# First layers of two pairs of edge blocks in one turn, and another head and end, in a graph network layer on one core

## The chip, the cores and the metric

One core of a Trainium2 chip. PE multiplies matrices into PSUM, DVE (vector) and ACT (scalar) work on tiles in SBUF and PSUM, POOL (GpSimd) here mostly issues gathers from DRAM, SP issues plain DMAs. The metric is the time of one execution on the device in microseconds; lower is better. Before the change it is 2216.37 us, the median of three runs (2215.54 to 2216.93).

## The reference

6250 nodes with 256 features, 206,250 directed edges sorted by target node, an average of 33 per node. Each edge has 64 raw features and one "polarity".

```python
h = relu(layernorm(x))
polarity = clip(edge_attr[:, 0:1], 0, 1)
e = relu(raw @ W_e1.T + b_e1) @ W_e2.T + b_e2            # raw: 64 features
edge_emb = (e * (polarity + 0.01)) @ W_le.T + b_le
msg = relu(h[src] + edge_emb)
aggr = segment_sum(msg, dst)                             # 6250 rows
g = (h + aggr) @ W_g1.T + b_g1
out = x + relu(layernorm(g) * ln_g + ln_b) @ W_g2.T + b_g2
```

All of it is float32. The kernel multiplies W_e2 and W_le into one matrix first (`wc_s`, with `bc_s` for the bias), so each edge passes through a first layer of 64 x 256 and a second of 256 x 256.

## The kernel before

**Tiles.** Edges are laid out in 67 groups of 3072 (6 blocks of 512) and one last group of a single block, 403 blocks in all. Two blocks are a *pair* (202 pairs): their raw features fill 128 partitions, the even block the upper 64 rows, the odd block the lower 64. Half a block, 256 edges, is a *unit* u; there are 806.

**What is done for a pair, and where.**
- `load_pair(q)` (L217): 256 KB of raw features by SP.
- `first_layer(q)` (L222): four matmuls with 64 rows (two blocks, two halves of the 256 features), the two blocks side by side in the upper and lower rows of the array; each result is a PSUM buffer of 128 x 512. It is evacuated with bias and relu by ACT (L241); for the first blocks only (L237), the last of the four goes to DVE (L238). Each matmul in float32 is two instructions on PE, so a first layer is 8 of them.
- `edge_part(u)` (L248): the second layer, four matmuls of 128 x 128 by 128 x 256 (8 instructions); DVE adds `bc_s` into `msg` (L261); a few early units (`plain`) are copied by ACT.
- `gathers` (L495): for each unit two indirect DMAs on POOL fetch the rows of `hb_d` (relu of the normalized x, plus b_le) into `hg`, one of 16 buffers. The first of each batch waits for the second layer's last matmul (`last_z`).
- `whole(u)` (L520): two multiply-adds on DVE (message times polarity plus gathered row, L526), a relu on ACT (L528), in place in `hg`.
- `add_up(b)` (L530): sums over edges with the same target, as matmuls with 0/1 matrices `sel` that have 32 columns; four of them lie side by side in the columns of the array (L536). They gather in `pd`; at the end of a group ACT copies them to `ms` (L542).
- `node_work(w)` (L569) for each of 49 windows of 128 nodes, in steps some units apart: `spread` loads, `ready` (L593) makes the normalized rows, `rows_of` (L599) takes the sums from the groups that touch the window (L607), `one`, `two`, `three` call `first`, `second`, `third` (L158 to L188) of `finish_nodes`.

**Order.** The order is written out by hand (`manual_schedule`): each engine runs its instructions as the program lists them. `forward(u)` (L275) emits the second layer of a unit; in one unit of four (u % 4 == TURN, that is 1) it also calls `turn_of(q)` (L268): the first layer of pair q + 2, then the sums that are due (`add_pairs`), then the load of pair q + 4. So PE goes through second layer (32 instructions), first layer (8), sums (16), and again. `whole` follows the second layer at a distance of 22 units that shrinks by one in every 36 units; `add_pairs` takes pairs whose units are all `whole`.

**PSUM.** Seven buffers `pz` of one bank each rotate among first layer, second layer and node work; `pd` is the eighth.

**Head.** The weights' product, the normalization of all x (in 13 parts: statistics on DVE, scaling on ACT, an add on POOL, stores to `hb_d` by SP) and the first 22 units of both layers run together; then the gathers start. In `todo`, keyed by unit, stand small early jobs: target rows, selection matrices, node weights, and a check of the edges' order whose verdict would send the kernel into a slow general version (`any_order`), which does not run here.

**End.** The last sums, `ms`, then the node work of the last two windows, as one chain.

Of the kernel before, what the change touches and what calls it, by code (L numbers as in the profile page):

```python
# [17 lines left out]
P = 128  # L18
# [23 lines left out]
SHRINK = 36  # L42
HG = 16
TURN = 1
CH = 4
# [46 lines left out]
def gnn_kernel(ctx: ExitStack, tc: tile.TileContext, x, src_c, dst_c, dst_r, pol_c, raw_t, w_e1t, w_e2,  # L92
# [49 lines left out]
    def finish_nodes(nd, ps, w, n):  # L142

        r = w * P

        def turn(a):
            pt = ps()
            for c in range(2):
                nc.tensor.transpose(pt[:, 0, c * P:c * P + n], a[:n, c * P:(c + 1) * P], ident[:n, :n])
            aT = nd.tile([P, 2, P], F32, name="aT")  # L150
            if n == P:
                nc.scalar.activation(aT, pt[:, 0, :].rearrange("p (c n) -> p c n", c=2), AF.Copy)
            else:
                for c in range(2):
                    nc.scalar.activation(aT[:, c, :n], pt[:, 0, c * P:c * P + n], AF.Copy)
            return aT

        def first(aT):  # L158
            ph = ps()
            for c in range(2):  # L160
                nc.tensor.matmul(ph[:n, 0, :], aT[:, c, :n], wg1_s[:, c, :], start=c == 0, stop=c == 1)  # L161
            hs = nd.tile([P, D], F32, name="hs")
            nc.vector.tensor_add(hs[:n], ph[:n, 0, :], bg1_b[:n])
            mv = row_stats(nd, n, 1, lambda i: hs[:n])
            rs = nd.tile([P, 1], F32, name="rs1")
            one_over_std(rs[:n], mv, n)
            nc.vector.tensor_scalar(hs[:n], hs[:n], mv[:n, 0, 0:1], rs[:n], op0=ALU.subtract, op1=ALU.mult)
            return hs

        def second(hs):  # L170
            pt = ps()
            for c in range(2):
                nc.tensor.transpose(pt[:, 0, c * P:c * P + n], hs[:n, c * P:(c + 1) * P], ident[:n, :n])  # L173
            nT = nd.tile([P, 2, P], F32, name="nT")
            for c in range(2):
                nc.scalar.activation(nT[:, c, :n], pt[:, 0, c * P:c * P + n], AF.Relu, bias=lnb_s[:, c:c + 1],  # L176
                                     scale=lng_s[:, c:c + 1])
            return nT

        def third(nT, xt):  # L180
            po = ps()
            for c in range(2):
                nc.tensor.matmul(po[:n, 0, :], nT[:, c, :n], wg2_s[:, c, :], start=c == 0, stop=c == 1)  # L183
            ot = nd.tile([P, D], F32, name="ot")
            nc.vector.tensor_add(ot[:n], po[:n, 0, :], bg2_b[:n])
            nc.vector.tensor_add(ot[:n], ot[:n], xt[:n])
            for a, b in spread_out(n):
                nc.sync.dma_start(out=out[bass.ds(r + a, b - a), :], in_=ot[a:b])  # L188

        def load_x():  # L190
            xt = nd.tile([P, D], F32, name="xt3")
            for a, b in spread_out(n):
                nc.sync.dma_start(out=xt[a:b], in_=x[bass.ds(r + a, b - a), :])
            return xt

        return turn, first, second, third, load_x

# [3 lines left out]
    with fast:  # L201
# [3 lines left out]
        sel_p = big.enter_context(tc.tile_pool(name="sel", bufs=3))  # L205
        e1_p = big.enter_context(tc.tile_pool(name="e1", bufs=6))
        msg_p = big.enter_context(tc.tile_pool(name="msg", bufs=LEAD + 2))
# [14 lines left out]
        def first_layer(q):  # L222
# [12 lines left out]
            for c in range(2):  # L235
                for s, b in enumerate(bs):
                    if b < 2 * LEAD // 4 + 4 and s == c == 1:  # L237
                        nc.vector.tensor_scalar(e1[b][:, c, :], pe[s, c], be1_s[:, c:c + 1], 0.0, op0=ALU.add,  # L238
# [9 lines left out]
        def edge_part(u):  # L248
# [4 lines left out]
            for i in range(2):  # L253
                k = (2 * v + i) * P
                for c in range(2):
                    last_z = nc.tensor.matmul(pz[:, i, :], e1[b][:, c, k:k + P], wc_s[:, c, :], start=c == 0, stop=c == 1)  # L256
            msg[u] = msg_p.tile([P, 2, D], F32, name="msg")
            if plain(u):
# [6 lines left out]
        last_z = None  # L265
        sums = lambda: None

        def turn_of(q):  # L268

            if q + 2 < NP:  # L270
                first_layer(q + 2)
            sums()
            load_pair(q + 4)

        def forward(u):  # L275

            edge_part(u)
            if u % 4 == TURN:
                turn_of(u // 4)

        nc.vector.memset(eps_t, EPS)
        nc.vector.memset(ones, 1.0)
        nc.vector.memset(rs_s, 0.0)
        nc.vector.memset(nm_s, 0.0)
        make_identity(nc, ident)
        warm = const.tile([P, 1], F32, name="warm")
        nc.scalar.activation(warm, eps_t, AF.Sqrt, bias=eps_t)
        vecs = load("vecs", [P, 8], vec_c, nc.scalar)
        be1_s, be2_s, lng_s, lnb_s = (vecs[:, 2 * i:2 * i + 2] for i in range(4))
        load_pair(0)  # L290
        nc.scalar.dma_start(out=we1_s, in_=w_e1t)
        early = ExitStack()
# [17 lines left out]
        with tc.tile_pool(name="p1", bufs=4) as p1, tc.tile_pool(name="p1x", bufs=11) as p1x:  # L310
# [52 lines left out]
            def offset():  # L363
# [5 lines left out]
                nc.scalar.activation(bc_s, pw, AF.Copy)  # L369

            load_rows(0, 2)
            rows_b = const.tile([P, 3, D], F32, name="rows_b")
            nc.scalar.dma_start(out=rows_b, in_=row_v.rearrange("(o r) d -> o r d", o=1).to_broadcast([P, 3, D]))
            ble_b, bg1_b, bg2_b = (rows_b[:, i, :] for i in range(3))
            load_rows(1)
            load_pair(1)
            load_rows(2)
# [9 lines left out]
            for k in range(len(parts) + 1):  # L387
# [19 lines left out]
                if k in lists:  # L407
                    t, src = lists[k]
                    nc.scalar.dma_start(out=t, in_=src[:, :NT])
            for u in units:  # L410
                forward(u)
# [77 lines left out]
        with tc.tile_pool(name="hg", bufs=HG) as hg_p, tc.tile_pool(name="ms", bufs=5) as ms_p, \  # L489
# [30 lines left out]
            def whole(u):  # L520

                m = msg.pop(u)
                if plain(u):
# [6 lines left out]
            def add_up(b):  # L530

                g = group_of(b)
                k = b - g * L
                for j in range(S):
                    m = hg[2 * b + j // 2]
                    nc.tensor.matmul(pd[j * W:(j + 1) * W, g % 2, :], sel[g][:, k * S + j, :], m[:, j % 2, :],  # L536
                                     start=k == 0, stop=b == blocks_of(g)[-1])
                hg.pop(2 * b)
                hg.pop(2 * b + 1)
                if b == blocks_of(g)[-1]:  # L540
                    ms[g] = ms_p.tile([P, D], F32, name="ms")
                    nc.scalar.activation(ms[g], pd[:, g % 2, :], AF.Copy)  # L542
                    sel.pop(g)
# [25 lines left out]
            def node_work(w, spread_now=False):  # L569
# [3 lines left out]

                far_apart = (3, 5, 4) if gs[-1] < NG - 3 else (2, 3, 2)
                turn, first, second, third, load_x = finish_nodes(nd, ps, w, n)

                def spread():
# [7 lines left out]
                    for g in gs:  # L585
# [3 lines left out]
                        box["sel2"].append(s2)  # L589
                    if not spread_now:  # L590
                        at(now + 3, ready)

                def ready():  # L593

                    hT, st = box["hT"], box["st"]
                    for i, op in enumerate((ALU.mult, ALU.add)):
                        nc.vector.tensor_tensor(hT[:, :, :n], hT[:, :, :n], st[:, i:i + 1, :n].to_broadcast([P, 2, n]), op)  # L597

                def rows_of():  # L599

                    if spread_now:
                        ready()
                    hT = box["hT"]
                    pa = ps()
                    for c in range(2):
                        for i, g in enumerate(gs):
                            nc.tensor.matmul(pa[:, c, :n], ms[g][:, c * P:(c + 1) * P], box["sel2"][i][:, :n],  # L607
                                             start=i == 0, stop=i == len(gs) - 1)
                    nc.vector.scalar_tensor_tensor(hT[:, :, :n], hT[:, :, :n], 0.0, pa[:, :, :n], op0=ALU.max, op1=ALU.add)
                    at(now + far_apart[0], one)  # L610

                def one():
                    box["hs"] = first(box["hT"])
                    at(now + far_apart[1], two)
# [21 lines left out]

            gathers(HG)
            nc.vector.tensor_copy(dst_f, dst_f.bitcast(I32))
            sums = add_pairs
            for i, fn in enumerate((first_rows, rows_of_edges, lambda: select(0), lambda: select(1), row_numbers,  # L640
                                    node_weights, stats_out)):
                at(LEAD + i, fn)
            for i, fn in enumerate((by_group(0, ALU.max), by_group(1, ALU.min), by_row(0, ALU.max), by_row(1, ALU.min),
                                    verdict, count, total)):
                at(LEAD + 22 + 2 * i, fn)
            flag = None
            for u in range(LEAD, NU):
                now = u
                forward(u)

                gathers(4 * summed + HG - 4 + (u - TURN) % 4 + 1, last_z)
                while made < u + 1 - max(LEAST, LEAD - u // SHRINK):
                    whole(made)
                    made += 1
                due()
                if u == NU - 10:
                    for w in range(NW):
# [20 lines left out]
def any_order(tc, dram, v):  # L678
# [7 lines left out]
    with tc.tile_pool(name="sc", bufs=1) as sc, tc.tile_pool(name="sk", bufs=2) as sk, \  # L686
# [78 lines left out]
        def nodes(w, n):  # L765
            ac = sk.tile([P, D], F32, name="ac_a")
            nc.sync.dma_start(out=ac[:n], in_=acc_d[bass.ds(w * P, n), :])
            turn, one, two, three, load_x = v["finish_nodes"](sk, lambda: sp1.tile([P, 1, D], F32, name="ps_a"), w, n)
            three(two(one(turn(ac))), load_x())

# [66 lines left out]
```

## Time and profile before

The profiled execution took 2216.74 us, 0.4 above the median; its span, from first to last instruction, is 2214.7 us.

| engine, line | what | times | busy us | mean ns |
|---|---|---|---|---|
| PE L256 | second layer | 6448 | 1477.7 | 382 |
| PE L233 | first layer | 1612 | 403.6 | 617 |
| PE L536 | sums | 3224 | 215.0 | 385 |
| PE L607 | sums to windows | 560 | 70.8 | 275 |
| DVE L526 | message times polarity plus row | 1612 | 703.5 | 477 |
| DVE L261 | bias of the second layer | 799 | 549.6 | 688 |
| ACT L528 | relu of the message | 806 | 511.2 | 634 |
| ACT L241 | evacuation of the first layer | 799 | 483.2 | 686 |
| whole span | | | 2214.7 | |

"Busy" is the time in which at least one instruction of the group was under way, so overlapping matmuls count once while their mean is that of one. The means of PE's rows cannot be multiplied by their number: matmuls in different rows or columns of the array run together, and those that follow each other overlap. What a stretch of PE costs is read from start to start in the timeline. The DMA engines are busy 44% in most of the span, at some 140 GB/s; only in the first fortieth are they full (95%, 307 GB/s). PE's granted clock is 0.998 of full speed over the span.

The page names what ended each idle time; for POOL, whose gathers are each followed by 0.30 us without any instruction, "issue" or whatever engine last signalled is named even when nothing was waited for.

### The profile page before, as it was taken

What the parts mean: (1) busy time and instruction counts of PE and PEld (TensorE: products, weight loads), DVE (VectorE), ACT (ScalarE), POOL (GpSimd) and SP (SyncE); (2) the same over time, 40 slices, a digit from 0 to 9 for tenths busy, and PEclk for the clock granted to TensorE, in tenths of its full rate; (3) what the DMA queues carried; (4) which work ended last, traced back from release to release, by engine and by line L of the source; (5) the groups of instructions that cost most, each with busy time, mean ns of one, the idle gap of its engine ahead of it and who ended that gap; (6) DMA issues with size and microseconds to landing.
All of it is one profiled execution on the core that took longest, in us unless ns stands there. A gap on an engine that the chain in (4) does not pass through costs nothing.

```text
span 2214.7 us, 33981 instructions
## 1 busy us (share of the span) xinstructions
PE 2189.4 (99%) x12360; PEld 1581.9 (71%) x12360; DVE 1477.9 (67%) x3277; ACT 1064.6 (48%) x1895; POOL 1639.9 (74%) x1674
## 2 busy tenths in 40 slices
PE   8999999999999999999999999999999999999998
PEld 6767777777777777777777776777777777777775
DVE  7786666666666666666667666666666666666665
ACT  7444454444444444444444444444444444454443
POOL 5777777777777777777777777777777777777773
PEclk9999999999999999999999999999999999999999
DMA  9544444444544444444444444444344444444442
GB/s 307 159 129 121 151 146 130 139 128 142 149 143 125 131 146 134 151 132 136 141 142 130 150 124 146 131 148 134 115 146 145 119 130 146 140 141 130 139 132 59
DMA packets 156070, 309.13 MB, mean 140 GB/s; under 512 B 33183, under 2 KB 77944, under 8 KB 155896
## 3 DMA queue, kind: packets, MB, share of 16 engines
q0 software_dynamic: 77376, 211.39, 32.5%
q1 hardware_dynamic: 77384, 92.24, 13.2%
q10 hardware_dynamic: 1136, 3.27, 0.5%
q8 instruction: 98, 1.61, 0.3%
q14 instruction: 76, 0.62, 0.1%
HBM read 293.92 MB, written 12.85 MB: 139 GB/s over the span
## 4 chain that ended last, share of the span: by engine, by line
PE 95%; DMA 1%; POOL 1%; DVE 1%; issue 1%; ACT 1%; SPq 0%; ACTq 0%; DVEq 0%
PE pz L256 62%; PE pz L233 17%; PE pd L536 9%; PE pz L607 3%; PE pz L183 2%; PE pz L161 2%; POOL hg L503 1%; DMA hg<-hb_d,src_s 1%; DVE hg L526 1%; PE pz L173 0%; ACT e L241 0%; DMA raw<-in_raw_t_dram 0%; DVE msg L261 0%; DMA wle_s<-in_w_let_dram 0%; ACT hg L528 0%
## 5 line engine op out<-in xcount | busy, mean ns | idle before, releaser
L503 POOL DMA_INDIRECT hg<-hb_d,src_s x1612 | 1604.1, 995 | 516.7 <-issue 350.2
L256 PE MATMUL pz<-wc_s,e 128*128 128x256 f32 x6448 | 1477.7, 382 | 3.4 <-DVE msg L261 1.7
L256 PEld LDWEIGHTS pz<-wc_s,e 128*128 128x128 f32 x6448 | 1200.8, 190 | 240.1 <-issue 49.4
L528 ACT ACTIVATE hg<-hg 128x512 f32<-128x512 f32 x806 | 511.2, 634 | 997.6 <-DVE hg L526 994.4
L261 DVE TENSOR_TENSOR msg<-pz,bc_s 128x512 f32<-128x512 f32 x799 | 549.6, 688 | 655.6 <-PE pz L256 655.3
L526 DVE SCALAR_TENSOR_TENSOR hg<-msg,pol_s,hg 128x256 f32<-128x256 f32 x1612 | 703.5, 477 | 22.5 <-DMA hg<-hb_d,src_s 21.9
L241 ACT ACTIVATE e<-pz,vecs 128x512 f32<-128x512 f32 x799 | 483.2, 686 | 108.0 <-PE pz L233 107.3
L233 PE MATMUL pz<-raw,we_s 64*128 64x512 f32 x1612 | 403.6, 617 | 6.4 <-DMA we_s<-in_w_e1t_dram 4.9
L233 PEld LDWEIGHTS pz<-raw,we_s 64*128 64x128 f32 x1612 | 139.9, 186 | 169.1 <-issue 137.0
L536 PE MATMUL pd<-hg,sel 128*32 128x256 f32 x3224 | 215.0, 385 | 3.9 <-ACT ms L542 3.9
L536 PEld LDWEIGHTS pd<-hg,sel 128*32 128x32 f32 x3224 | 84.5, 109 | 187.6 <-issue 134.8
L607 PEld LDWEIGHTS pz<-s,ms 128*128 128x128 f32 x560 | 70.1, 192 | 3.9 <-ACT ms L542 0.9
L607 PE MATMUL pz<-s,ms 128*128 128x128 f32 (+1 forms) x560 | 70.8, 275 | 0.7 <-ACT ms L542 0.7
L516 DVE TENSOR_TENSOR sel<-iota_w,rel 128x768 f32<-128x768 f32 x68 | 63.8, 938 | 0.0
L347 POOL TENSOR_TENSOR hb<-xt,rows_b 128x256 f32<-128x256 f32 (+1 forms) x49 | 34.2, 732 | 25.4 <-ACT xt L343 17.2
L183 PE MATMUL pz<-wg_s,nT 128*128 128x256 f32 (+1 forms) x196 | 51.4, 386 | 0.0
L161 PE MATMUL pz<-wg_s,hT 128*128 128x256 f32 (+1 forms) x196 | 50.1, 379 | 0.0
L597 DVE TENSOR_TENSOR hT<-hT,stb 128x256 f32<-128x256 f32 (+1 forms) x98 | 41.2, 421 | 1.7
L183 PEld LDWEIGHTS pz<-wg_s,nT 128*128 128x128 f32 (+1 forms) x196 | 37.5, 192 | 6.0 <-PE pd L536 0.4
L161 PEld LDWEIGHTS pz<-wg_s,hT 128*128 128x128 f32 (+1 forms) x196 | 37.1, 190 | 5.1
L176 ACT ACTIVATE nT<-pz,vecs 128x128 f32<-128x128 f32 (+1 forms) x98 | 38.8, 446 | 0.6 <-PE pz L173 0.6
L587 DVE TENSOR_SCALAR s<-iota_p,rowid 128x128 f32<-128x128 f32 x140 | 31.8, 291 | 0.0
(76 smaller groups left out, 326.3 us busy)
## 6 DMA issues: line engine op xcount, KB each, us to landing
raw<-in_raw_t_dram SPq DMA_DIRECT2D x202, 256.0 KB, 3.0
hg<-hb_d,src_s POOLq DMA_INDIRECT x1612
stb<-st_d SPq DMA_DIRECT2D x49, 128.0 KB, 5.6
hb_d<-hb SPq DMA_DIRECT2D x12, 512.0 KB, 5.1
xt<-in_x_dram SPq DMA_DIRECT2D x48, 128.0 KB
hT<-in_x_t_dram SPq DMA_DIRECT2D x48, 128.0 KB
out_dram<-ot SPq DMA_DIRECT2D x48, 128.0 KB, 2.6
xt<-in_x_dram SPq DMA_DIRECT2D x11, 512.0 KB, 9.3
```

Of the source, the lines that this page charges most:

```text
L161: nc.tensor.matmul(ph[:n, 0, :], aT[:, c, :n], wg1_s[:, c, :], start=c == 0, stop=c == 1)
L183: nc.tensor.matmul(po[:n, 0, :], nT[:, c, :n], wg2_s[:, c, :], start=c == 0, stop=c == 1)
L233: nc.tensor.matmul(pe[s, c], we1_s[s * F:(s + 1) * F, c * P:(c + 1) * P], raw[q][s * F:(s + 1) * F, :], start=True, stop=True)
L241: nc.scalar.activation(e1[b][:, c, :], pe[s, c], AF.Relu, bias=be1_s[:, c:c + 1])
L256: last_z = nc.tensor.matmul(pz[:, i, :], e1[b][:, c, k:k + P], wc_s[:, c, :], start=c == 0, stop=c == 1)
L261: nc.vector.tensor_add(msg[u], pz, bc_s)
L503: g = nc.gpsimd.indirect_dma_start(out=hg[u][:, i, :], out_offset=None, in_=hb_d, in_offset=bass.IndirectOffsetOnAxis(ap=src_s[:, 2 * u + ...
L516: nc.vector.tensor_tensor(sel[g][:, :n, :], iota_w.rearrange("p (o w) -> p o w", o=1).to_broadcast([P, n, W]), rel[:, t:t + n].rearrange(" ...
L526: nc.vector.scalar_tensor_tensor(hg[u][:, i, :], m[:, i, :], pol_s[:, 2 * u + i:2 * u + i + 1], hg[u][:, i, :], op0=ALU.mult, op1=ALU.add)
L528: nc.scalar.activation(hg[u], hg[u], AF.Relu)
L536: nc.tensor.matmul(pd[j * W:(j + 1) * W, g % 2, :], sel[g][:, k * S + j, :], m[:, j % 2, :], start=k == 0, stop=b == blocks_of(g)[-1])
L607: nc.tensor.matmul(pa[:, c, :n], ms[g][:, c * P:(c + 1) * P], box["sel2"][i][:, :n], start=i == 0, stop=i == len(gs) - 1)
```

## The change

- **Turns.** For pairs 6 to 195 (`by_two`, `FEW = 6`), a turn with even q does the first layers of pairs q + 2 and q + 3 and then sums; a turn with odd q only sums. The two loads that belong to them also come together. At both ends of the kernel the turns stay as before. `e1` gets 8 buffers instead of 6. In this stretch `whole` is held back by one unit ahead of each turn.
- **Evacuation.** The last of the four results of a first layer goes to DVE for every pair.
- **Head.** Nine products of a tile of ones with itself on PE; the first layer's weights are loaded before the vectors; pair 1 is loaded before the rows of x. The cast of the target list moves from DVE to POOL, ahead of the first gather. The early jobs are spaced differently, the check of the order over five units a step instead of two.
- **End.** The last two units skip the message tile: DVE multiplies straight from PSUM, and `bc_s` times polarity is added to the gathered rows at unit 803. The last group's sums go to a `pz` buffer, and the last two groups' copies to DVE. The last windows' work starts at unit 789 instead of 796, with `ready` in steps of its own; the sums of earlier groups come first in `rows_of`. For windows that end in the last two groups, `first` adds the bias by a one-row matmul and DVE reads PSUM directly.
- **Every window.** The output's bias is added to x in `ready` (`offset`), so `third` has one add instead of two. The second part of an output (the last window) is issued by ACT.

```diff
+FEW = 6
...
-        def first(aT):
+        def first(aT, bias_by_pe=False):
             ph = ps()
+            if bias_by_pe:
+                nc.tensor.matmul(ph[:n, 0, :], ones[0:1, :n], bg1_b[0:1], start=True, stop=False)
...
-            nc.vector.tensor_add(ot[:n], po[:n, 0, :], bg2_b[:n])
-            nc.vector.tensor_add(ot[:n], ot[:n], xt[:n])
+            nc.vector.tensor_add(ot[:n], po[:n, 0, :], xt[:n])
...
-                    if b < 2 * LEAD // 4 + 4 and s == c == 1:
+                    if s == c == 1:
...
+        def by_two(q):
+            return FEW <= q < NP - FEW
+
         def turn_of(q):
-            if q + 2 < NP:
+            if not by_two(q):
+                if q + 2 < NP:
+                    first_layer(q + 2)
+            elif q % 2 == 0:
                 first_layer(q + 2)
-            sums()
-            load_pair(q + 4)
+                first_layer(q + 3)
+            sums(q == NP - 1)
+            if not by_two(q):
+                load_pair(q + 4)
+            elif q % 2 == 0:
+                load_pair(q + 4)
+                load_pair(q + 5)
...
+            if pz is not None:
+                for i in range(2):
+                    m = hg[u][:, i, :]
+                    nc.vector.scalar_tensor_tensor(m, pz[:, i, :], pol_s[:, 2 * u + i:2 * u + i + 1], m, op0=ALU.mult,
+                                                   op1=ALU.add)
+                    nc.scalar.activation(m, m, AF.Relu)
...
+        for _ in range(9):
+            nc.tensor.matmul(ps()[:, 0, :P], ones, ones, start=True, stop=True)
...
+            load_pair(1)
             load_rows(0, 2)
...
-            load_pair(1)
             load_rows(2)
...
+            nc.gpsimd.tensor_copy(dst_f, dst_f.bitcast(I32))
...
-            nc.vector.tensor_copy(dst_f, dst_f.bitcast(I32))
             sums = add_pairs
-            for i, fn in enumerate((first_rows, rows_of_edges, lambda: select(0), lambda: select(1), row_numbers,
-                                    node_weights, stats_out)):
+            for i, fn in ((0, first_rows), (1, rows_of_edges), (3, lambda: select(0)), (5, row_numbers), (6, stats_out),
+                          (7, lambda: select(1)), (8, node_weights)):
...
-                at(LEAD + 22 + 2 * i, fn)
+                at(LEAD + 22 + 5 * i, fn)
...
-                while made < u + 1 - max(LEAST, LEAD - u // SHRINK):
+                while made < u + 1 - max(LEAST, LEAD - u // SHRINK) - (by_two(u // 4) and (u + 1) % 8 in (TURN, TURN + 4)):
...
+                if u == NU - 3:
+                    for k in range(2 * NU - 4, 2 * NU):
+                        m = hg[k // 2][:, k % 2, :]
+                        nc.vector.scalar_tensor_tensor(m, bc_s[:, 0, :], pol_s[:, k:k + 1], m, op0=ALU.mult, op1=ALU.add)
-                if u == NU - 10:
+                if u == NU - 17:
```

## The prediction

> **What bounds the kernel now.** I read the page's busy times first, then the costliest groups, then the timeline of PE in a steady stretch, then POOL's gathers, and the head and the end last.
>
> ```profile
> PE 2189.4 (99%) x12360; PEld 1581.9 (71%) x12360; DVE 1477.9 (67%) x3277; ACT 1064.6 (48%) x1895; POOL 1639.9 (74%) x1674
> ```
> ```profile
> L503 POOL DMA_INDIRECT hg<-hb_d,src_s x1612 | 1604.1, 995 | 516.7 <-issue 350.2
> ```
>
> PE is busy 99% of the span, so the bound is PE; but a busy PE need not be streaming. And POOL, at 74%, has far less slack than that: each of its 1612 gathers is followed by about 0.30 us in which nothing is seen, 484 of the 516.7 us of idle, so only some 33 us of POOL's time from 65.7 to 2182.8 us is real waiting. The timeline of PE in a steady stretch:
>
> ```profile
> 1000.80 1.99 PE L233 MATMUL pz<-raw,we_s 64*128 64x512 f32 x8
> 1002.72 1.07 PE L536 MATMUL pd<-hg,sel 128*32 128x256 f32 x16
> 1003.72 5.45 PE L256 MATMUL pz<-wc_s,e 128*128 128x256 f32 x24
> ...
> 1013.60 1.07 PE L536 MATMUL pd<-hg,sel 128*32 128x256 f32 x16
> 1014.60 7.17 PE L256 MATMUL pz<-wc_s,e 128*128 128x256 f32 x32
> 1021.71 1.99 PE L233 MATMUL pz<-raw,we_s 64*128 64x512 f32 x8
> ```
>
> Start to start, a first layer (x8) takes 1.92 us, the sums (x16) 1.00, the 32 second-layer instructions 7.11: 10.03 us a pair, back to back. The loads of the first layer's weights show its pace once it runs:
>
> ```profile
> 1001.33 0.19 PEld L233 LDWEIGHTS pz<-raw,we_s 64*128 64x128 f32 x2 [0.24 <-issue]
> 1001.76 0.19 PEld L233 LDWEIGHTS pz<-raw,we_s 64*128 64x128 f32 x2 [0.24 <-issue]
> ```
>
> Two instructions (the two row halves) run together and the next two follow 0.43 us later. Four such steps are 1.72 us; the block takes 1.92. **0.20 us** of each first layer is the price of having entered its tiling. The chain of waits says the same of the whole: 95% PE. Only from 66 to about 155 us does it run through the gathers and DVE; there, from 100 to 200 us, PE idles 5.3 us (30.0 - 28.25 and 70.0 - 66.44 by stage).
>
> **The change, part by part.**
>
> *First layers of two pairs in one turn.* The built program has 107 blocks of first layers instead of 202: 95 double ones, the blocks of sums (195) as before. A double block is 8 steps, 3.44 us, plus one entry. The saving is at most 95 x 0.20 = **19.0 us**; it is nothing if PE has to wait inside the double block. That depends on PSUM: eight results in seven rotating buffers. The eighth result takes the buffer of the first. ACT's four evacuations take 2.42 us in one row, so 0.605 each, and the first starts 1.23 us into the block (2.03 - 0.80): it is done at 1.84, and the eighth result starts at 0.20 + 6 x 0.43 = 2.78. Spare 0.9 us. The seventh takes the buffer of the unit just before the block, which DVE empties 0.8 us after the block starts, if its queue is not behind. The sums behind the block need relus queued four units (9 us) earlier, because the change holds one `whole` back ahead of each turn. I take the full 19.0.
>
> *One evacuation in four from ACT to DVE.* In before this is so only for the first seven pairs (0.75 us, row below). It adds about 194 x 0.75 = 145 us to DVE: 1478 + 145 = 1623, 74% of the new span. In the queue behind it stand `whole`'s two multiplies. The cover is a hole that is there already, in the timeline of DVE:
>
> ```profile
> 1005.75 0.69 DVE L261 TENSOR_TENSOR msg<-pz,bc_s 128x512 f32<-128x512 f32 x1 [3.37 <-PE pz L256]
> ```
>
> DVE waits 3.37 us in each turn while PE does first layer and sums; a double block makes one such hole longer and puts 1.5 us into it. Cost on PE nothing. The cost that remains is on POOL, which is nearly full.
>
> Here a rule speaks against the change. The Trainium skill, "SBUF — State Buffer", section "Who interferes with whom": DVE and GpSimd share one pair of ports; a `tensor_scalar` can take both ports and then GpSimd is blocked for the whole instruction, descriptor writing included. The trace shows such a case: the first gather runs beside the two clean-ups of the polarity and takes twice its usual time.
>
> ```profile
> 65.56 0.99 DVE L412 TENSOR_SCALAR pol_s<-pol_s 128x1612 f32<-128x1612 f32 x1
> 65.67 2.03 POOL L503 DMA_INDIRECT hg<-hb_d,src_s  x1 [3.65 <-DVE msg L261]
> ```
>
> And an evacuation of a first layer on DVE, as the head of the kernel has it:
>
> ```profile
> 8.45 0.75 DVE L238 TENSOR_SCALAR e<-pz,vecs 128x512 f32<-128x512 f32 x1 [7.22 <-PE pz L233]
> ```
>
> If the new evacuations, also `tensor_scalar`, lock POOL each time, that is up to 145 us of POOL time and a kernel about 100 us slower. The same section limits the rule to 2-port modes and two SBUF inputs, and the rows fit the limit: 1612 columns in 0.99 us are 0.61 ns each, the evacuation from PSUM takes 0.75 / 512 = 1.46 ns each, so it is not in the fast mode. For the price I use this trace: gathers have a median of 949 ns and a mean of 995, 74 us of stretching over 1478 us of DVE work, 0.05 us for each us. So 145 x 0.05 = **7 us** of POOL time.
>
> *POOL's margin after that.* Real waiting 33 us, and a gather issued about 15 us before its use at the end where some 4 are needed (a landing is 2.7 to 4.0 us in the chain): 33 + 11 = 44. Used up: 19 by a faster PE, 7 by stretching. 18 are left, so PE still bounds, but the stretch in which gathers decide (to 155 us now) lasts longer. I charge **+1.5**; ends 0 and +10.
>
> *The early jobs.* The cast of dst (1.00 us) leaves DVE for POOL, the range checks are put every 5 units instead of 2, and the selections are apart. They lie in the stretch where DVE and gathers decide, with 5.3 us of PE idle. Ends 0 and -5; I take **-1**, since the gathers' own pace (0.95 + 0.30 us) sets most of it. The cast stands on POOL ahead of the first gather, and every gather waits behind it. No row shows it: DVE takes 1.00 us, POOL's two-input add 0.68 us for 256 columns would give 4.3. I take 2.5. POOL's last add ends at 62.0 and the first gather starts at 65.7, held by the landing of the last store of hb: 3.65 us of cover. Cost nothing, 0.7 at the upper end.
>
> *The head*, in the timeline of PE:
>
> ```profile
> 4.89 3.49 PE L233 MATMUL pz<-raw,we_s 64*128 64x512 f32 x8 [4.89 <-DMA we_s<-in_w_e1t_dram]
> 8.71 1.97 PE L356 MATMUL pz<-wle_s,we_s 128*128 128x256 f32 x8 [0.32 <-DMA we_s<-in_w_e_dram]
> 12.13 1.99 PE L233 MATMUL pz<-raw,we_s 64*128 64x512 f32 x8 [1.46 <-DMA raw<-in_raw_t_dram]
> 14.05 1.99 PE L368 MATMUL pz<-wle_s,be_b 128*128 128x256 f32 x8
> 15.88 3.62 PE L256 MATMUL pz<-wc_s,e 128*128 128x256 f32 x16
> ```
>
> The nine products of ones warm PE up: the first layer at 4.89 runs 3.49 us against 1.99 later. That 1.5 us alone buys little, as the product still waits for its weights until 8.7. What pays is that the second pair is loaded ahead of the rows of x: its first layer follows the product at 8.7 + 1.8 = 10.5 instead of 12.13. So the second layer starts at about 14.3, **1.6 us** earlier, and DVE, which waited 2.26 us for that first layer, starts its statistics as much earlier; the last store of hb, and the first gather, move with it. Ends -0.5 (x's rows arrive 0.8 us later, 256 KB at 307 GB/s) and -2.5. Second-layer work on the same queues is otherwise unchanged.
>
> *The end.* From the last second-layer instruction (2192.8) to the end there are 21.9 us. Gone from the chain of waits, of which these are pieces: one bias add in `first` for each of two windows and one add in `third` (0.45 each).
>
> ```profile
> 2200.99 0.44 DVE hs L163
> ...
> 2208.40 0.43 DVE ot L185
> 2208.83 0.02 issue
> 2208.86 0.42 DVE ot L186
> ```
>
> The message add of the last two units goes too, but four multiplies (4 x 0.43) and an offset (0.42) now stand in DVE's queue beside units 803 to 805, where it has 1.2 us of gaps, and PE gets a one-row matmul (0.43) ahead of each `first`. Net **-1.2**, ends -2.5 and +0.5.
>
> Sum: -19.0 + 1.5 - 1.0 - 1.6 - 1.2 = -21.3. The profiled execution took 2216.7 (span 2214.7), so 2195.4; the median lies 0.4 below that execution: **2195 us**.
>
> **The rivals.**
> (a) *Gathers take over* (18%). For: until 1238 us POOL shows no wait beyond its 0.30; 1.30 us a gather is nearly PE's pace. Against: the 18 us of margin. If half the merging is lost to DVE waiting for gathers: 2205 us.
> (b) *PSUM* (7%). PE waits 0.2 us or more for the seventh or eighth buffer in each double block because DVE's queue runs late (the node work of one window is some 4 us of DVE rows). The 19 us are gone: 2214, no change that can be told.
> (c) *The new evacuations block POOL* (7%): slower. Place: POOL, from the first double turn on. Price: if each us on DVE stretches gathers by 0.5 us, 73 us on a POOL that has 44 and gives 19 to PE: 73 - 25 = 48, against a PE path of 2195: 2243 us. It turns slower than before from about 0.32 us for each us (46 / 145).
> (d) *The early stretch melts* (5%): its 5.3 us and the upper ends of head and end all come: 2188.
>
> **How the numbers follow.** Likeliest (63%): 2195, its own range 2190 to 2200. The range reaches to (d) below and takes in (a): 2187 to 2209, which leaves (b) and (c) out. This kernel's measurement tells 0.2%, 4.4 us, from no change. Faster is the likeliest with (a) and (d): 0.86; (b) is no change, 0.07; (c) slower, 0.07.
>
> **What would show it.** Double blocks of x16 that take 3.64 us from first layer to sums, sums alone between second layers in the other turns; wrong if they take 3.8 or more or if PE waits for ACT or DVE inside them. Mean gather still under 1.01 us and median 0.95; at 1.03 and more, (c) acts. DVE's waits for gathers grow past 22 us under (a). The second layer starts near 14.3, the first gather near 64. The prediction falls if PE's idle time grows by more than 8 us in all.

## The result and the profile after

The changed kernel takes **2199.97 us** (median of six runs, 2196.54 to 2201.03), the kernel before 2216.65 beside it (2215.32 to 2218.10): ratio **0.9921**, 95% interval 0.9911 to 0.9932. The profiled execution took 2199.43 us with a span of 2197.7, so 17.0 us of span are gone where 21.3 were forecast. Of the kernels tried below, the last two (pair 1 later, no ones) ran where the kernel before takes 2215.9 us; the ten ahead of them ran where it took 2516 to 2546 us itself, from a cause that no run shows.

The profile page of the changed kernel, busy times and groups (busy us and mean ns; after the second bar the idle time just before and what ended it):

```profile
PE 2181.4 (99%) x12382; PEld 1599.7 (73%) x12382; DVE 1619.1 (74%) x3473; ACT 975.7 (44%) x1701; POOL 1641.8 (75%) x1675
...
L536 POOL DMA_INDIRECT hg<-hb_d,src_s x1612 | 1604.6, 995 | 499.7 <-issue 348.7
...
L561 DVE SCALAR_TENSOR_TENSOR hg<-msg,pol_s,hg 128x256 f32<-128x256 f32 x1608 | 687.6, 478 | 14.2 <-DMA hg<-hb_d,src_s 13.8
...
L243 PE MATMUL pz<-raw,we_s 64*128 64x512 f32 x1612 | 381.8, 606 | 3.4 <-DVE msg L273 3.3
L248 DVE TENSOR_SCALAR e<-pz,vecs 128x512 f32<-128x512 f32 x201 | 150.7, 750 | 193.8 <-PE pz L243 193.8
```

The first layers' busy time fell by 21.8 us, from 403.6. DVE has its 201 evacuations of 0.75 us, and a gather still takes 995 ns in the mean. The timeline of PE where the prediction showed it:

```profile
1004.70 3.71 PE L243 MATMUL pz<-raw,we_s 64*128 64x512 f32 x16
1008.34 1.07 PE L572 MATMUL pd<-hg,sel 128*32 128x256 f32 x16
1009.34 7.17 PE L266 MATMUL pz<-wc_s,e 128*128 128x256 f32 x32
1016.44 1.07 PE L572 MATMUL pd<-hg,sel 128*32 128x256 f32 x16
```

From start to start the double block takes 3.64 us where two single ones took 2 x 1.92 = 3.84: 0.20 saved, and the next turn has no first layer at all.

So where are the missing 4.3 us? Not in the steady stretch. Two double blocks, near 92 and 225 us, wait for several us. The timeline of PE at the first (the bracket is idle time and what ended it):

```profile
92.41 1.99 PE L243 MATMUL pz<-raw,we_s 64*128 64x512 f32 x8
94.96 1.12 PE L243 MATMUL pz<-raw,we_s 64*128 64x512 f32 x2 [0.56 <-DVE msg L273]
97.22 3.26 PE L243 MATMUL pz<-raw,we_s 64*128 64x512 f32 x6 [1.14 <-DVE msg L273]
```

and the chain of waits through the same place (start, us, what):

```profile
87.74 6.05 DMA hg<-hb_d,src_s
...
93.82 0.03 DVE hg L561
...
94.22 0.68 DVE msg L273
...
96.47 0.70 DVE msg L273
...
97.22 3.26 PE pz L243 x6
100.48 1.86 PE pd L572 x16
```

Read together: a gather issued at 87.74 lands 6 us later; `whole` (L561) waits for it on DVE; the message adds (L273) that would empty PSUM buffers stand in the queue behind it; and PE, in the middle of a double block that needs eight results, has no free buffer. The block takes 8.0 us instead of 3.64. Then sums take 1.86 us instead of 1.00: PE runs at half clock, granted from 97.8 to 104.6 us. The second such block:

```profile
225.08 2.84 PE L243 MATMUL pz<-raw,we_s 64*128 64x512 f32 x10
229.13 1.12 PE L243 MATMUL pz<-raw,we_s 64*128 64x512 f32 x2 [1.22 <-DVE msg L273]
230.60 1.84 PE L243 MATMUL pz<-raw,we_s 64*128 64x512 f32 x4 [0.34 <-DVE msg L273]
232.37 1.93 PE L572 MATMUL pd<-hg,sel 128*32 128x256 f32 x16
```

and the chain through it, behind a gather that took 6.97 us to land:

```profile
225.40 0.03 DVE hg L561
...
225.80 0.68 DVE msg L273
226.49 0.37 DVE hg L561
...
226.87 0.48 DVE hg L561
227.35 0.34 DVE xt L204
227.69 0.35 DVE hT L636
...
228.06 0.42 DVE hT L636
228.48 0.60 DVE msg L273
229.08 0.87 DVE sel L549
229.95 0.61 DVE msg L273
...
230.60 1.84 PE pz L243 x4
```

Here not only the late gather stands ahead of the message adds, but also DVE's own work between them: the multiplies (L561), a window's node work (L204, L636) and a selection matrix (L549), from 226.49 to 228.48 and from 229.08 to 229.95. The clock is at half from 230.9 to 234.3. In the kernel before, it is full from 8.0 to 2206.1 us. Of the 95 double blocks 92 take 3.63 to 3.64 us; three (at 92.4, 160.1 and 225.1 us) exceed it, by 4.4, 1.2 and 3.7 us. Not each of these waits is a loss against the kernel before, which idles in this stretch too; the table of units at the end of the experiments tells which one is.

### The profile page after: what moved, and what is told of

Read it like the earlier page. It is cut to its first block, busy times and chain, and to the rows that moved or that the text cites. A ratio compares the mean times of both kernels' runs of the same rounds, so it can differ in the third digit from the quotient of the medians.

```text
span 2197.7 us, 34900 instructions
## 1 busy us (share of the span) xinstructions
PE 2181.4 (99%) x12382; PEld 1599.7 (73%) x12382; DVE 1619.1 (74%) x3473; ACT 975.7 (44%) x1701; POOL 1641.8 (75%) x1675
## 4 chain that ended last, share of the span: by engine, by line
PE 93%; DVE 1%; POOL 1%; DMA 1%; issue 1%; ACT 0%; SPq 0%; POOLq 0%; DVEq 0%; ACTq 0%
PE pz L266 61%; PE pz L243 16%; PE pd L572 9%; PE pz L656 3%; PE pz L190 2%; PE pz L164 2%; POOL hg L536 1%; DMA hg<-hb_d,src_s 1%; PE pz L180 0%; DVE hg L561 0%; DVE msg L273 0%; DMA hb_d<-hb 0%; DVE hT L636 0%; PE pz L647 0%; DVE far L493 0%
## 5 line engine op out<-in xcount | busy, mean ns | idle before, releaser
L536 POOL DMA_INDIRECT hg<-hb_d,src_s x1612 | 1604.6, 995 | 499.7 <-issue 348.7
L273 DVE TENSOR_TENSOR msg<-pz,bc_s 128x512 f32<-128x512 f32 x797 | 546.6, 688 | 317.2 <-PE pz L266 316.4
L561 DVE SCALAR_TENSOR_TENSOR hg<-msg,pol_s,hg 128x256 f32<-128x256 f32 x1608 | 687.6, 478 | 14.2 <-DMA hg<-hb_d,src_s 13.8
L251 ACT ACTIVATE e<-pz,vecs 128x512 f32<-128x512 f32 x605 | 361.6, 691 | 219.2 <-PE pz L243 218.7
L243 PE MATMUL pz<-raw,we_s 64*128 64x512 f32 x1612 | 381.8, 606 | 3.4 <-DVE msg L273 3.3
L248 DVE TENSOR_SCALAR e<-pz,vecs 128x512 f32<-128x512 f32 x201 | 150.7, 750 | 193.8 <-PE pz L243 193.8
L243 PEld LDWEIGHTS pz<-raw,we_s 64*128 64x128 f32 x1612 | 148.9, 187 | 181.6 <-issue 154.7
L656 PE MATMUL pz<-s,ms 128*128 128x128 f32 x548 | 69.0, 275 | 0.0
L549 DVE TENSOR_TENSOR sel<-iota_w,rel 128x768 f32<-128x768 f32 x68 | 63.8, 938 | 0.0
L579 ACT ACTIVATE ms<-pd 128x256 f32<-128x256 f32 x66 | 25.3, 383 | 57.3 <-PE pd L572 56.7
L636 DVE TENSOR_TENSOR hT<-hT,stb 128x256 f32<-128x256 f32 (+1 forms) x98 | 41.7, 426 | 1.7
```

The lines of the kernel that those rows point to most:

```text
L243: nc.tensor.matmul(pe[s, c], we1_s[s * F:(s + 1) * F, c * P:(c + 1) * P], raw[q][s * F:(s + 1) * F, :], start=True, stop=True)
L251: nc.scalar.activation(e1[b][:, c, :], pe[s, c], AF.Relu, bias=be1_s[:, c:c + 1])
L273: nc.vector.tensor_add(msg[u], pz, bc_s)
L536: g = nc.gpsimd.indirect_dma_start(out=hg[u][:, i, :], out_offset=None, in_=hb_d, in_offset=bass.IndirectOffsetOnAxis(ap=src_s[:, 2 * u + ...
L561: nc.vector.scalar_tensor_tensor(hg[u][:, i, :], m[:, i, :], pol_s[:, 2 * u + i:2 * u + i + 1], hg[u][:, i, :], op0=ALU.mult, op1=ALU.add)
```

## The experiments

In the traces of the first ten kernels, instructions of DVE and ACT keep their durations and gathers land as before (by the packets' records about 2.5 us from the start of their issue in the median, 2.46 in the changed kernel). But PE pauses between matmuls without a wait that the profile names (without double turns 78 such pauses ahead of second-layer matmuls, 55 us in all, where the changed kernel has none), DVE and ACT often begin late after the matmul that they wait for (up to 10 us in the rows below; in the changed kernel DVE's message adds, when they wait, begin 0.04 us after it), and the granted clock is 0.93 to 0.97. These traces also hold only 16 to 21 thousand of the 40 thousand semaphore updates of the others, so that the names of what ended a wait are less sure in them. The ratios of these ten are therefore a test under late starts, not parts of the 0.9921, and the changed kernel itself is not among them.

**Double turns alone.** The kernel before with

```diff
-        e1_p = big.enter_context(tc.tile_pool(name="e1", bufs=6))
+        e1_p = big.enter_context(tc.tile_pool(name="e1", bufs=8))
...
+            elif q % 2 == 0:
+                first_layer(q + 2)
+                first_layer(q + 3)
...
```

> The kernel before with nothing but the double first layers (8 buffers of e1, loads in pairs, one `whole` held back); evacuation after the first seven pairs by ACT alone, head, early jobs and end as before. My terms: 95 entries x 0.20 = 19.0, less 1.5 for the thinner gather margin: 2216.6 - 17.5 = 2199, double blocks of x16 at 3.64 us from start to start. Rival PSUM: with ACT alone the sixth to eighth evacuations run later, the eighth result waits for its buffer and a double block takes 3.75 us or more: 2209 or slower. Rival 'the early stretch is what the merging costs': 4 us of the saving are lost before unit 120, 2202.

Measured 2626.15, ratio 1.0339 (1.0317 to 1.0361). **No double turns**, `FEW = 1000` in the changed kernel, twice:

> The changed kernel with FEW so large that no turn is double; head, end, early jobs and the evacuation by DVE remain. My terms: head -1.6, end -1.2, early jobs -1.0: 2216.6 - 3.8 = 2212.8. If the loss before unit 120 belongs to the early jobs and not to the double turns, the stretch at half clock near 100 us is here too and the kernel is only 0 to -1.5 from before, 2215 to 2216.5. If it belongs to the double turns, PE stays at full clock and the time is 2212 to 2213.

> The changed kernel with no double turns once more (on the chip of the first four runs every kernel, the one before too, was 15% slower, because PE's signals to the other engines came late in bursts, and the double turns lost 3.4%). On a chip where the kernel before takes 2216, my terms give head -1.6, end -1.2, early jobs -1.0: ratio 0.9983 (2212.8). If the loss before unit 120 belongs to the early jobs, the stretch at half clock near 100 us is here too and the ratio is 0.9993 to 1.0. On the slow chip: ratio 1.000 as before.

Ratios 1.0007 (0.9995 to 1.0019) and 0.9996 (0.9984 to 1.0007). Under late starts all of the loss belongs to the double turns, and head, end, early jobs and DVE's evacuation together bring nothing that can be told, against 0.9983 expected. No kernel without double turns ran beside a kernel before of 2216 us; what they bring there is read from the rows.

**Evacuation by ACT.**

```diff
-                    if s == c == 1:
+                    if b < 2 * LEAD // 4 + 4 and s == c == 1:
```

> The changed kernel with all evacuations but those of the first seven pairs on ACT. My term: the evacuations on DVE stretch POOL by 7 us, which its margin hides: 2200, no change within 2 us; mean of a gather stays 0.995. Rival (they lock POOL): the mean falls below 0.95 and the kernel is 5 us or more faster. Rival PSUM: without DVE's help ACT's evacuations come too late and double blocks stretch by 0.1 us or more each: 2209 or slower.

Ratio 1.0254 (1.0228 to 1.0280). Gathers average 1017 ns here, and 1015 and 1020 in two kernels that ran beside it with the evacuations on DVE: 3 ns x 1612 = 5 us at most, not the 73 of the prediction's rival (c).

**The loads near 88 us**, one and then both hunks:

```diff
-(5, row_numbers), (6, stats_out), (7, lambda: select(1)), (8, node_weights)
+(2, node_weights), (5, row_numbers), (6, stats_out), (7, lambda: select(1))
...
-            elif q % 2 == 0:
-                load_pair(q + 4)
-                load_pair(q + 5)
+            else:
+                load_pair(q + 4)
```

> The changed kernel with the loads of the node weights (512 KB) issued at unit 24 instead of 30, ahead of the first double turn; nothing else. Theory 'burst': at 85 to 89 us SP issues 1.4 MB (statistics, node weights, two pairs of raw features, the first window's loads) in front of which the gathers land after 6 us instead of 3; DVE stands behind them, PE idles and the clock falls to half. Without the weights in it the landing falls under 4.5 us, the stretch at half clock from 97.8 to 104.6 us is gone, and the kernel gains 2 to 4 us: 2197. Rival 'pace': gathers come at 1.25 us each and set the time there anyway: no change, 2200.

> The changed kernel with the node weights' loads at unit 24 instead of 30, once more. On a chip where the kernel before takes 2216: theory 'burst' (1.4 MB of loads issued in 4 us hold the gathers up, 6 us to land instead of 3) gives a gain of 2 to 4 us over the changed kernel, ratio 0.990 to 0.991, no half clock before 110 us; rival 'pace' (POOL's 1.25 us for each gather sets that stretch anyway) gives 0.992, as the changed kernel. On the slow chip the ratio is above 1.03 and neither is told apart.

> The changed kernel with the burst at 85 to 89 us taken apart in two ways: the node weights (512 KB) loaded at unit 24, and the second pair's raw features of a double turn loaded one turn later (256 KB a turn instead of 512 KB every other). Theory 'burst': the landing of 6 us near 88 us and of 7 us near 218 us, and the stretches at half clock behind them, go; 3 to 5 us faster than the changed kernel, ratio to before 0.990. Rival 'pace' (POOL's 1.25 us a gather sets the time there): ratio 0.992 as the changed kernel, PE idle near 88 to 110 us as before. On a chip where the kernel before takes 2500 us or more: ratio above 1.02, and only the stretch before 90 us can be read.

Ratios 1.0369, 1.0295 and 1.0304: the times tell nothing apart. From the packets' records, the seven or eight gathers issued between 85 and 95 us land in the mean 3.7 us after the start of their issue in the changed kernel and 3.9 without double turns, but 3.2 to 3.3 in these three. So the burst holds gathers up by half a microsecond; whether that is what lets the block at 92 us run dry is left open.

**Double turns only from pair 34 on** (`34 <= q < NP - FEW`).

> The changed kernel with double turns only from pair 34 on (unit 136) instead of pair 6: 14 doubles fewer. If PE sets the time everywhere, that costs 14 x 0.20 = 2.8 us against the changed kernel: ratio to before 0.9934. If POOL's pace of 1.30 us a gather sets the time until about unit 120, the early doubles bring nothing: 0.992, as the changed kernel. If the early doubles are what makes PE wait long enough to lose its full clock (97.8 and 230.9 us), leaving them out gains 2 to 4 us: 0.990 to 0.991. On a chip where the kernel before takes 2500 us or more none of these is told apart; there the 14 doubles fewer of 95 should take about a seventh off the 3% by which the changed kernel is slower.

Ratio 1.0297 (1.0259 to 1.0334). A seventh off would be 0.4%, less than the spread of the kernels with all double turns (1.0254 to 1.0369): nothing told apart.

**Why double turns lose there.** The timeline of `e1_merge_only`, PE, DVE and ACT around one double block:

```profile
1210.29 2.84 PE L234 MATMUL pz<-raw,we_s 64*128 64x512 f32 x10
1212.83 0.69 DVE L262 TENSOR_TENSOR msg<-pz,bc_s 128x512 f32<-128x512 f32 x1 [2.91 <-PE pz L234]
1213.58 1.12 PE L234 MATMUL pz<-raw,we_s 64*128 64x512 f32 x2 [0.45 <-DVE msg L262]
1219.21 0.69 DVE L262 TENSOR_TENSOR msg<-pz,bc_s 128x512 f32<-128x512 f32 x1 [5.68 <-remote]
...
1219.95 2.68 PE L234 MATMUL pz<-raw,we_s 64*128 64x512 f32 x3 [5.25 <-issue]
1220.68 1.84 ACT L242 ACTIVATE e<-pz,vecs 128x512 f32<-128x512 f32 x3 [10.04 <-remote]
```

PE has put out six results (each is two instructions); ACT starts to empty the first of them 10 us after the block began; PE stands for 5.25 us. Two kernels test whether it is the number of buffers: the one without double turns and `bufs=4` instead of 7 in `psz`, and double turns with the sums put between the two first layers.

> The changed kernel with no double turns and 4 rotating PSUM buffers instead of 7. By the clean trace the fourth result of a first layer then has 0.7 us to spare (it takes the buffer of the unit just before, which DVE empties 0.8 us after the block starts, and starts itself 1.5 us into it), about the spare of a double block with 7 buffers (0.9). Theory 'depth': double turns lose on these chips because PE's signals come late by several us and PE runs dry of free buffers; then this kernel loses too, ratio 1.02 to 1.04, with the waits inside first layers. Rival 'other parts' (loads in pairs, the `whole` that is held back, 8 buffers of e1): all of these are absent here, ratio 1.000 as without double turns and 7 buffers.

> The changed kernel with the two first layers of a double turn kept in the same turn, but the sums between them: loads in pairs, `whole` held back, e1 with 8 buffers, 4 results and then 4 more, 7 buffers. No entry into the tiling is saved. Theory 'depth': with the sums (1 us) between, fewer results are due at once, so most of the 3% goes: ratio 1.000 to 1.012. Rival 'other parts': all of them are here, so the loss stays: 1.02 or more. On a chip where the kernel before takes 2216: 0.998 to 1.000, as without double turns.

Four buffers: ratio 1.0682 (1.0644 to 1.0719), more than expected. Apart: 1.0159 (1.0132 to 1.0187), about half of the loss, between the two expectations. The rows of PE's first layer, page by page: no double turns and 7 buffers (`e5_no_merge_2`),

```profile
L243 PE MATMUL pz<-raw,we_s 64*128 64x512 f32 x1612 | 438.1, 624 | 30.9 <-DVE msg L273 13.7
```

no double turns and 4 buffers (`e9_four_buffers`),

```profile
L243 PE MATMUL pz<-raw,we_s 64*128 64x512 f32 x1612 | 598.1, 660 | 132.8 <-DVE msg L273 80.8
```

double turns and 7 buffers (`e7_no_burst`):

```profile
L243 PE MATMUL pz<-raw,we_s 64*128 64x512 f32 x1612 | 501.8, 659 | 149.6 <-DVE msg L273 95.5
```

and apart (`e10_apart`):

```profile
L243 PE MATMUL pz<-raw,we_s 64*128 64x512 f32 x1612 | 468.9, 639 | 37.2 <-DVE msg L273 16.1
```

Fewer buffers without a double turn give the idle time of a double turn (132.8 us against 149.6, and 30.9 with neither): under late starts a lack of free PSUM buffers is enough to make first layers wait. It is not all of the loss. In "apart" that idle time is down to 37.2 us, yet half of the 3% stays; the two first layers so near to each other, or the other parts of the double turn, cost something too, and these were not separated.

**The head**, both beside a kernel before of 2215.9 us. Pair 1 loaded later:

```diff
-            load_pair(1)
             load_rows(0, 2)
...
             load_rows(1)
+            load_pair(1)
```

> The changed kernel with the load of pair 1 back behind the first two loads of rows of x, as in the kernel before. Only the first 65 us are read. My step (what pays in the head is that pair 1 is loaded ahead of the rows): its first layer waits for its load again and runs from about 11 to 12 us instead of 9.4 to 9.9; the second layer starts at 15.0 to 15.6 (13.2 to 14.1 with it), and the first gather about 0.8 us later than in the changed kernel, near 65.2. Rival (the products of ones and the earlier load of the first layer's weights pay): the second layer still starts before 14.2.

The timeline of PE in this kernel:

```profile
7.58 1.97 PE L388 MATMUL pz<-wle_s,we_s 128*128 128x256 f32 x8 [0.42 <-DMA we_s<-in_w_e_dram]
11.65 3.68 PE L243 MATMUL pz<-raw,we_s 64*128 64x512 f32 x8 [2.11 <-DMA raw<-in_raw_t_dram]
15.27 2.00 PE L400 MATMUL pz<-wle_s,be_b 128*128 128x256 f32 x8
17.10 1.24 PE L266 MATMUL pz<-wc_s,e 128*128 128x256 f32 x5
```

The second layer starts at 17.10 us, 3.5 later than in the changed kernel (13.62): PE waits 2.1 us for the load and then runs that first layer at half clock (granted from 11.8 to 15.2 us), 3.68 us instead of 1.99. My step holds against the rival, but the start is later than my 15.0 to 15.6, because I had not counted the clock. The first gather comes at 66.85 instead of 64.06. Yet the time is 2199.76, ratio 0.9921 (0.9904 to 0.9937), that of the changed kernel.

Without the nine products of ones (the loop is deleted):

> The changed kernel without the nine products of ones. Only the first 65 us are read. My step (the warm first layer of pair 0 alone buys little, since the product waits for its weights anyway): the first layer takes 3.5 us instead of 2.1 again, and the second layer starts at most 0.5 us later than in the changed kernel, by 14.2. Rival (the warm start pays in full): 1.2 to 1.5 us later, 15 or more.

```profile
4.38 3.78 PE L243 MATMUL pz<-raw,we_s 64*128 64x512 f32 x8 [4.38 <-DMA we_s<-in_w_e1t_dram]
8.09 2.99 PE L386 MATMUL pz<-wle_s,we_s 128*128 128x256 f32 x8
11.01 1.99 PE L243 MATMUL pz<-raw,we_s 64*128 64x512 f32 x8
...
14.76 3.62 PE L266 MATMUL pz<-wc_s,e 128*128 128x256 f32 x16
```

Second layer at 14.76, 1.1 us later than in the changed kernel: neither my 0.5 nor in full. The product does not wait for its weights here; it starts behind a cold first layer and is itself half cold (2.99 us against 1.97). The time, 2198.51, ratio 0.9916 (0.9899 to 0.9932), is again that of the changed kernel.

These two are also the changed kernel twice over in the stretch that matters. Counted in the traces (eight second-layer instructions a unit), how much earlier a unit starts than in the kernel before, in us, at units ahead of which PE has done the same work (at unit 70 but for two small matmuls of the check):

| unit | changed kernel | pair 1 later | no ones | double turns so far |
|---|---|---|---|---|
| 22 | 1.48 | -1.22 | 1.11 | 0 |
| 70 | 3.05 | -0.29 | 1.98 | 6 |
| 120 | -0.11 | -1.00 | 1.06 | 12 |
| 200 | 1.90 | 1.01 | 3.07 | 22 |
| 805 | 17.34 | 16.44 | 18.50 | 95 |

From unit 120 to 805 all three gain 17.4 us: 83 double blocks at 0.20 are 16.6, and one wait of PE for ACT's copy of `ms` became 0.8 us shorter (1.30 us at 1382.6 before, 0.53 at 1470.5 in the changed kernel).

From 22 to 120 they gain -1.6, 0.2 and -0.05, where 12 double turns should give 2.4. In all three the same three double blocks exceed 3.63 us by more than 1 us; the first in the kernel without the ones:

```profile
92.78 1.99 PE L243 MATMUL pz<-raw,we_s 64*128 64x512 f32 x8
96.02 1.12 PE L243 MATMUL pz<-raw,we_s 64*128 64x512 f32 x2 [1.26 <-DVE msg L273]
98.29 3.22 PE L243 MATMUL pz<-raw,we_s 64*128 64x512 f32 x6 [1.14 <-DVE msg L273]
```

Behind it the two head kernels lose the full clock for 6.8 us (from 100.5 and 98.9 us). Yet this block costs next to nothing in the end: by unit 70 (197 us in the changed kernel) the three have gained 1.6, 0.9 and 0.9 us since unit 22, where six double turns are 1.2. The kernel before loses as much there in another place: its PE idles 5.3 us between 112 and 158 us, the changed kernel's 0.1.

What stays lost lies between units 70 and 120: -3.2, -0.7 and -0.9 us where six more double turns should give 1.2, so 4.4, 1.9 and 2.1 are missing. There stands the third block, at 225.1, 228.4 and 226.2 us; it is 3.7, 2.1 and 2.3 us too long (the single blocks of the kernel before, at 220.1 and 230.1 us, take 1.92 each), and only in the changed kernel's profiled execution is the clock at half behind it, which costs about 1 us more (1.86 us for the next sums instead of 1.00). In the kernel without the ones the chain into this block does not come from a gather at all, but from PE's own second layer, which ends at 226.23 and which a message add follows at 226.25. From there the same DVE work stands in the queue as shown above (multiplies, `xt`, `hT`, a selection), and PE starts its last four instructions at 231.02. So 2 us of this wait are DVE's own queue; the late gather and the clock make up the rest in the changed kernel.

No kernel here is faster than the changed one beyond the intervals. No run kept a window's node work and a selection out of the queue of a double block, which is what the third block suggests.

## Why the prediction was right, and where it was off

The direction, the size and the mechanism held: 2199.97 lies in the likeliest case's own range (2190 to 2200) at its very edge, 5 us above the forecast. By terms, for the profiled execution:

| term | forecast | measured | from |
|---|---|---|---|
| double blocks | -19.0 | -19.0 | 95 x 0.20, rows |
| gather margin and early jobs | +0.5 | +3.1 | units 22 to 805 gain 15.9, not 19.0: -0.4 to unit 70, +4.4 to 120, -0.8 behind it |
| head | -1.6 | -1.5 | unit 22 |
| end | -1.2 | +0.3 | unit 805 to the end: 23.99 us, 23.70 before |
| sum | -21.3 | -17.1 | span: -17.0 |

**The mis-sized term is the early stretch**: +1.5 for the gather margin less 1.0 for the early jobs. I charged late gathers as a delay of their own and let PSUM hold everywhere ("if its queue is not behind"). In three of 95 blocks DVE's queue was behind: at 92.4 us because of a late gather, at 160.1 us because of a window's node work, at 225.1 us because of both. Node work in DVE's queue is the reason that I gave for rival (b). Only the last of the three stays a loss, 4.4 us with what stands behind it. And a loss of clock, which I had nowhere, came on top: 6.8 + 3.4 us at half clock in the profiled execution, of which the second part counts. In the six runs of the changed kernel the one with a granted clock of 0.999 took 2196.54 us, the five with 0.996 or 0.997 took 2198.6 to 2201.0. Where the 3.1 were 1.3 and 1.6 (the two head kernels: 19.0 less 17.7 and 17.4), the clock was lost once in this stretch. What holds DVE up is read from the chains; no run removed it beside a kernel before of 2216 us.

**Head**: its size at unit 22 was right, and so were the first gather (64.06 us) and the cast on POOL (1.53 us, hidden). The second layer started earlier than forecast (13.62 against 14.3), because I had put the warm start at next to nothing. But little of the head is kept: with pair 1 later it is 2.7 us worse at unit 22, 3.3 at unit 70 and 0.9 from unit 120 on. The third block waits for DVE, so that most of PE's lead is waited away there.

**End**: from the last sums (2180.05) to the last add (2191.74) it is 11.7 us instead of 12.9, but not because of the adds. The three removed adds take 1.3 us out of the chain; PE's one-row matmuls, the normalizing steps that now read PSUM (0.54 and 0.56 us instead of 0.41 and 0.42) and the longer last sums put about 1.1 back. What is left, 1.0 us, is the clock: the last eight instructions of PE took 2.77 us before, where half clock was granted from 2206.1 us, and take 1.74 now, where it is granted only from 2193.6, behind them. In the chain of the kernel before and of the changed one:

```profile
2205.60 2.77 PE pz L183 x8
...
2189.56 1.74 PE pz L190 x8
```

In the two head kernels it fell to half ahead of them (2189.5 and 2187.9 us), and the end there takes 25.1 and 25.0 us, 1.4 and 1.3 longer than before. The four multiplies and the offset (L713, L204) now stand in DVE's queue ahead of the last sums, which start 6.4 us after unit 805 instead of 5.4; and the store takes 5.9 us to the span's end instead of 5.4. My upper end of +0.5 held in the profiled execution, by the luck of the clock; my value of -1.2 was wrong in all three.

**DVE's 150 us** cost POOL nothing: the mean of a gather is 995 ns before and after, so my 7 us of stretching were not there, and rival (c), in which they block POOL, falls on the same row. It agrees with the limit in the Trainium skill, "SBUF — State Buffer", section "Who interferes with whom": outside the 2-port modes a DVE instruction with at most one input from SBUF does not contend with GpSimd, and these evacuations read PSUM at 1.46 ns a column. Rival (a) shows no sign either: DVE's waits for gathers fell from 22 to 14.2 us, PE's idle time from 25.3 to 16.3, and POOL keeps 499.7 - 484 = 16 us of real waiting of its 33.

**Rival (b)** was right as a mechanism, in one double block of 95 that counts instead of in each, and in a condition that I had not thought of. My spare of 0.9 us for the eighth result is enough while DVE and ACT begin at once; in the ten kernels where they begin several us late it is gone, and those with double blocks were 2.5 to 3.7% slower than the kernel before.

## What to carry to other kernels

A merged block saves its entries into the tiling only while all its results find a free PSUM buffer: work out the spare of the last result, and name each queue on which the emptying instruction can stand behind something else, a late gather or a rare but long piece of work. A gain on PE counts from the unit on at which PE sets the pace; ahead of it, a lead is waited away. A wait that the change brings is a loss only where the kernel before did not wait too: compare both at points of equal work. An add taken off the last chain helps only by what its replacement does not cost, in that chain and in the queues ahead of it.

## What the runs showed of the hardware

PE lost its full clock after short pauses: within 94.4 to 97.2 us it idled 0.56 and 1.14 us around the two instructions of one matmul, and at 97.8 us the granted clock fell to a half, for 6.8 us; with 1.26 and 1.14 us in the kernel without the ones the same at 98.9 us. Behind 1.22 and 0.34 us near 230 us it fell for 3.4 us; behind 0.57 and 0.34 us at the same block of the kernel without the ones it did not, nor in the kernel before behind single pauses of 0.83 to 1.57 us that lie some 11 us apart. The Trainium skill, "TensorE: Matmul & The Clock Gate", section "A second HAM failure mode: psum-queue depth-cycling", tells of such a case in another kernel: a PE that pauses often for PSUM loses its clock and regains it. Here two such pauses in 2.8 us went ahead of it.
